# Two-layer attention and MLP block on one core: the place of the memory keys' transposes in the preparation

## The chip, the core and the metric

The kernel runs on one core of a Trainium2 chip, as one launch. The metric is the time of one execution in microseconds (us), the median of three runs. The engines are named as the profile names them: PE (TensorE, matmuls; PEld is its weight load), DVE (VectorE), ACT (ScalarE), POOL (GpSimd) and SP (SyncE, whose queue issues all DMAs of this kernel).

## The reference

The input `x` has 8 batches of 512 tokens of 256 numbers, in float32. Two layers follow each other; each normalises `x` and adds two branches to it:

```python
xn = _layernorm(x)
x = x + attention(xn, Wq, Wk, Wv, pre_proj, post_proj, mem_k, mem_v, Wout, bout) + fp4_mlp(xn, w_gate, w_up, w_down)
xn = _layernorm(x)
x = x + gated_convolution_and_mlp(xn, Wg, Wi, A, Bp, Cp, Dp, gamma, ...) + int4_linear_with_lora(xn, kernel, bias, a, b)
```

The attention has 16 heads of 64. Its keys are 64 learned memory keys per head (`mem_k`) ahead of the tokens' own keys. The dot products of all heads are mixed by `pre_proj` (16x16), masked causally, cut to the 64 largest of each row (`top_k`), put through softmax, mixed by `post_proj`, and applied to the values. The first MLP quantises weights and activations to FP4 in blocks of 16; the second layer's linear part quantises its weight to INT4 with one scale, the maximum over the whole weight.

## The kernel before

The kernel has three stages. The first **prepares weights** and takes the first 117 us. The second, the **search stage**, runs the attention over 64 groups (8 batches times 8 groups of 64 queries) with the selection of the 64 largest keys as a search by counting. The third computes everything else of both layers. A test behind the search stage can send the kernel to an exact, slow path; with these inputs it is not taken.

*How the order is made.* The instructions of a stage are recorded by `Straight` (L165), whose calls all appear as line 235 in the profile, into a `Plan` (L81). `Plan.tails` (L99) gives each operation a due time, minus the costliest chain of work that hangs behind it, plus its `late` mark; `Plan.run` (L114) then places the operations on their engines one after the other by estimated costs, taking the most urgent of those that are ready. What comes out is a fixed order for every engine and for SP; on the chip each engine takes its queue in that order and waits where an operand is missing. `Straight.part` (L185) describes a tile access as one range of partitions and one range of columns, from the first to the last column that it touches; two accesses whose ranges overlap, one of them a write, are taken to depend on each other in the plan. Matmuls that follow each other into one PSUM bank are one operation of the plan. An operation's `after` list names operations that must be placed ahead of it.

*The preparation (L677 to L854).* Its parts are these:

- **Folding (L754 to L782).** The products of `Wq`, `Wk` and `pre_proj` are folded into one matrix `mg` (`mgm` for the memory keys), so that the search stage needs no separate projections. `bd` (L718) holds `Wk` and the memory keys spread in a block pattern of 20 blocks: blocks 0 to 15 hold `Wk`, copied by ACT and DVE, blocks 16 to 19 the transposed memory keys. The loop has 20 turns. Turn `j` has a first product (8 matmuls of `bd[:, c, j]` with `wq` into one of two banks `pa`), a copy to `both` (ACT for even turns, DVE for odd ones), a second product (4 matmuls with `kr`, which holds `pre_proj`, into one of three banks `pm`), a copy to `mg` and a square on ACT, and a sum of the squares on DVE (`sqp`). Turns 16 to 19 use the memory keys. From the sums comes `tot`, which the search stage starts from.
- **Memory keys (L730 to L741).** 8 transposes of `mk` on PE into one bank, and two DVE copies into `bd[rows, :, 16:, t, :]`. Their range of columns, as `part` sees it, reaches from block 16 of the first chunk to the end of the last one, over nearly all of `bd`. They are recorded ahead of the folding loop and marked `late = 30`.
- **First tokens and value weights (L786 to L845).** The first batch is normalised (DVE), transposed (8 on PE), and `Wv` and `Wout` are transposed (32 on PE), marked `late = 4`.
- **`prepare` (L365).** The FP4 weights go through `quantise` eight times, with two sets of tiles (`w_v0` and so on, `w_v1`): two loads of `w_gate` and `w_up` rows by DMA, the largest of each block on DVE (`w_amax`), a product on POOL, ACT and DVE steps, two more products on POOL into `w_lo`, and transposes of `w_lo` on PE. The last two quantise `w_down`. A set's next load waits for POOL's last product on it. The INT4 weight (`kernel`) is loaded into the place of `Wv`, and its maximum goes through one `partition_all_reduce` on POOL (L492), the only library instruction of the stage. Last, `w1s`, weights of the third stage, is stored by DMA (L514); the search stage's first tiles lie where `w1s` lay.

*The search stage's end of a group.* The last round of the search leaves in `raw` minus twice the number of keys above a threshold. L1209 makes `foff` from it on DVE, and `pick` (L1145) compares `foff` with the eight numbers in `io8` (L818) to choose which of the eight largest remaining values is the cut.

Of the kernel before, what the change touches and what calls it, by code (L numbers as in the profile page):

```python
# [11 lines left out]
ALU = mybir.AluOpType  # L12
# [7 lines left out]
H, DH = 16, 64  # L20
HC = H * DH // P
MEM = 64
# [4 lines left out]
GB = 8  # L27
# [15 lines left out]
AIM = LOW + 3.5  # L43
# [22 lines left out]
def keys(ib):  # L66

    return MEM + RB * (ib + 1)
# [528 lines left out]
def block_kernel(ctx: ExitStack, tc: tile.TileContext, a: dict, out: bass.AP):  # L597
    nc = tc.nc
# [4 lines left out]
    ident = const.tile([P, P], F32, name="ident")  # L603
# [42 lines left out]
    with ExitStack() as c0:  # L646
# [15 lines left out]
        io8 = keep.tile([P, 8], F32, name="io8")  # L662
        base = {}
# [13 lines left out]
        with tc.tile_pool(name="prep", bufs=1) as prep, tc.tile_pool(name="prep_ps", bufs=1, space=PSUM) as pps:  # L677
            pl = Plan({})
            r = Straight(nc, pl)
# [3 lines left out]
            def bank(kind):  # L683
                own = {"a": banks[:2], "m": banks[2:5], "t": banks[5:]}[kind]
                used[kind] = used.get(kind, -1) + 1
                return own[used[kind] % len(own)]
# [4 lines left out]
            mk = prep.tile([MEM, H, DH], F32, name="mk")  # L691
# [26 lines left out]
            bd = prep.tile([P, HC, NJ, 2, 16], F32, name="bd")  # L718
            r.gpsimd.memset(bd[:, : HC // 2], 0.0)
            r.vector.memset(bd[:, HC // 2 :], 0.0)  # L720
            for j0 in range(0, 16, 8):
                for t in range(2):
                    for i in range(2):
                        rows = slice(t * DH, (t + 1) * DH)
# [2 lines left out]
                            bd[rows, half, j0 : j0 + 8, t, :],  # L727
                            wkm[rows, half, j0 * 16 : (j0 + 8) * 16].rearrange("p c (j i) -> p c j i", i=16),
                        )
            r.late = 30.0  # L730
            ps = bank("t")
            for c in range(HC):
                r.tensor.transpose(
                    ps[:, c * MEM : (c + 1) * MEM],
                    mk[:, 2 * c : 2 * c + 2, :].rearrange("m h d -> m (h d)"),
                    ident[:MEM, :MEM],
                )
            for t in range(2):
                rows = slice(t * DH, (t + 1) * DH)
                r.vector.tensor_copy(bd[rows, :, 16:, t, :], ps[rows].rearrange("p (c j i) -> p c j i", c=HC, i=16))  # L740
            r.late = 0.0  # L741

            row16 = prep.tile([P, 16], F32, name="row16")
            r.vector.tensor_reduce(row16, ident.rearrange("p (k i) -> p i k", i=16), AX.X, ALU.add)
# [9 lines left out]
            for j in range(NJ):  # L754
                pa = bank("a")
                for i in range(2):
                    for u in range(4):
                        c = 4 * i + u
                        r.tensor.matmul(
                            pa[u * 32 : (u + 1) * 32, i * D : (i + 1) * D], bd[:, c, j].rearrange("p t i -> p (t i)"),  # L760
                            wq[:, c, :], start=True, stop=True,
                        )
                ab = both[j % 3]
                (r.scalar.copy, r.vector.tensor_copy)[j % 2](ab, pa)
                pm = bank("m")
                for e in range(DC):
                    for i in range(2):
                        r.tensor.matmul(
                            pm[:, e * D : (e + 1) * D], ab[:, i * D + e * P : i * D + (e + 1) * P],
                            kr[:, i].rearrange("p k i -> p (k i)"), start=(i == 0), stop=(i == 1),  # L770
                        )
                dst = mg[:, :, :, j * 16 : (j + 1) * 16] if j < 16 else mgm[:, :, :, (j - 16) * 16 : (j - 15) * 16]
                r.scalar.copy(dst, pm.rearrange("p (e k i) -> p e k i", e=DC, i=16))
                r.scalar.activation(junk[j % 2], pm, AF.Square)
                r.vector.tensor_reduce(sqp[:, j], junk[j % 2].rearrange("p (q i) -> p q i", i=16), AX.X, ALU.add)
# [5 lines left out]
            ps = bank("a")  # L781
# [19 lines left out]
            for e in range(DC):  # L801
                ps = bank("t")
# [12 lines left out]
                r.vector.tensor_reduce(cmask[:, c : c + 1], row[:, 0:c], AX.X, ALU.add)  # L815
            r.vector.tensor_scalar(cmask, cmask, MASKED, None, ALU.mult)
            for q in range(8):
                r.gpsimd.memset(io8[:, q : q + 1], 3.5 - q)  # L818
            for na, to in base.items():
                r.gpsimd.memset(to, -2.0 * AIM)  # L820
                for ib in range(NB):
# [6 lines left out]
            for c in range(0, HC, 2):  # L828
                ps = bank("t")
# [6 lines left out]
            for g in range(HC // 2):  # L836
                ps = bank("t")
# [234 lines left out]
        def count(g, s, cur, raw, b, on_act):  # L1072


            src = block(s, g, b)
            thr = cur[:, 0, b : b + 1]
            junk = wp.tile([P, WD[-1]], I8, name=f"junk{int(on_act)}")[:, : src.shape[-1]]
            if on_act:
                nc.scalar.activation(  # L1079
                    junk, src, AF.Sign, bias=thr, scale=-1.0, accum_out=raw[:, b : b + 1]  # L1080
                )
            else:
                nc.vector.scalar_tensor_tensor(  # L1083
                    junk, src, thr, two.to_broadcast([P, src.shape[-1]]), ALU.is_ge,
                    ALU.mult, accum_out=raw[:, b : b + 1],
                )
# [94 lines left out]
        def search(pl, g, s, w, deps, rounds):  # L1181

            def begin():
                w["cur"] = cur = st.tile([P, 2, GB], F32, name="cur", bufs=14)
                nc.gpsimd.tensor_copy(cur[:, 0], guess[:, g * GB : (g + 1) * GB])

            tail = pl.add("POOL", 0.4, begin, deps)
            for k, (na, on_pool) in enumerate(rounds):
                def open_():
                    w["raw"] = st.tile([P, GB], F32, name="raw", bufs=8)  # L1190

                counts = []
                tail = pl.add("none", 0.0, open_, [tail])
                for b in range(GB):
                    def one_count(b=b, na=na):
                        count(g, s, w["cur"], w["raw"], b, b < na)

                    n = keys(g * GB + b)
                    counts.append(
                        pl.add("ACT", 0.28 + 0.00083 * n, one_count, deps + [tail]) if b < na else  # L1200
                        pl.add("DVE", 0.17 + 0.00105 * n, one_count, deps + [tail])
                    )

                def step(k=k, na=na, on_pool=on_pool):
                    if k < len(ROUNDS) - 1:
                        narrow(g, w, k, na, on_pool)
                    else:
                        w["off"] = st.tile([P, GB], F32, name="foff", bufs=4)
                        nc.vector.tensor_scalar(w["off"], w["raw"], -0.5, -AIM, ALU.mult, ALU.add)  # L1209

                last = k == len(ROUNDS) - 1
                tail = pl.add(
                    "POOL" if on_pool else "DVE",
                    0.2 if last else (1.3 if k == 0 else 5.5) if on_pool else 1.8 if k < len(ROUNDS) - 2 else 2.1,
                    step, counts,
                )
                deps = []
            return tail
# [293 lines left out]
        for n, (b, g) in enumerate(groups):  # L1512
# [7 lines left out]
            if n % 2 == 0:  # L1520
                pair = ORDER[n % NG : n % NG + 2]
                q, qdone, stored = queries(pl, pair, o, xdone)
# [4 lines left out]
            w = {}  # L1527
# [55 lines left out]
        with tc.If(flag > 0):  # L1583
            nc.sync.dma_start(mgf, mg_d)
            nc.sync.dma_start(mgmf, mgm_d)
            with tc.For_i(0, B) as b:
# [4 lines left out]
                for n, g in enumerate(ORDER):  # L1591
                    if n % 2 == 0:
                        pair = ORDER[n : n + 2]
                        q, qdone, stored = queries(pl, pair, o, xdone)
# [13 lines left out]
                    w = {}  # L1608
# [21 lines left out]
    r = Straight(nc, pl)  # L1630
# [221 lines left out]
```

## Time and profile before

| | us |
|---|---|
| median of three runs (2841.61 to 2843.36) | 2842.69 |
| the profiled execution | 2840.84 |
| its span, from the first to the last instruction | 2839.1 |
| PE busy, 19064 matmuls | 2539.6 |
| DVE busy, 7978 instructions | 2439.3 |
| ACT busy | 2026.9 |
| POOL busy | 1206.7 |
| the preparation: PE's first instruction of the search stage starts at | 117.28 |
| PE, DVE and POOL busy in 0 to 117.28 | 79.87, 79.55 and 40.87 |
| DVE busy, L1209 (64 instructions) | 11.3 |

The profile is one execution seen by a hardware profiler. A row of its timeline gives the start, the length, the engine, the line, the operation, the tiles written and read, and how often it is repeated; in brackets stands how long the engine had been idle before it and what ended that idle time. "SPq" rows are DMAs being issued. A row of windows gives, for a stretch of time, each engine's busy time and its number of instructions.

### The profile page before, as it was taken

The numbers are of one execution on the slowest core, as the hardware profiler recorded it, in microseconds if no ns is written. First come the engines' busy times: TensorE is split into PE (matmuls) and PEld (weight loads), VectorE is DVE, ScalarE is ACT, GpSimd is POOL, SyncE is SP. The second block draws the span as 40 slices with busy tenths as digits, with TensorE's granted clock in tenths as the row PEclk, the third lists the DMA queues.
The fourth block names the chain that finished last, engine by engine and source line by source line (L and its number), as shares of the span: only waits on it lengthen the run. The fifth ranks groups of instructions, "written<-read, shape, count | busy, mean of one in ns | idle before, by whom it ended". The sixth has DMA issues, their size and how long they took to land. (4 is left out here: it accounts for less than half of the span.)

```text
span 2839.1 us, 57481 instructions
## 1 busy us (share of the span) xinstructions
PE 2539.6 (89%) x19064; PEld 1966.9 (69%) x19064; DVE 2439.3 (86%) x7978; ACT 2026.9 (71%) x5876; POOL 1206.7 (43%) x2215
## 2 busy tenths in 40 slices
PE   5999999999999999999999999999986578999997
PEld 3677777777777778777787777778765455666664
DVE  6678989989989998999899889999999969877762
ACT  3478887788788878887888788788897444644442
POOL 3203544345444544444453545455445344444320
PEclk9999999999999999999999999999987788999998
DMA  4300010100000000000000010000110031000000
GB/s 135 148 24 16 27 30 16 29 18 19 21 25 18 28 18 27 20 18 26 21 19 18 25 29 17 16 23 20 35 42 5 8 109 30 23 16 15 8 8 15
DMA packets 114871, 82.70 MB, mean 29 GB/s; under 512 B 79339, under 2 KB 108806, under 8 KB 113798
## 3 DMA queue, kind: packets, MB, share of 16 engines
q1 hardware_dynamic: 114566, 78.95, 9.1%
q8 instruction: 153, 2.51, 0.4%
q14 instruction: 152, 1.25, 0.1%
HBM read 44.04 MB, written 35.39 MB: 28 GB/s over the span
## 5 line engine op out<-in xcount | busy, mean ns | idle before, releaser
L1079 ACT ACTIVATE junk<-ring,cur 128x312 int8<-128x312 f32 (+27 forms) x1560 | 864.0, 560 | 32.9 <-POOL cur L1132 12.0
L1083 DVE SCALAR_TENSOR_TENSOR junk<-ring,cur,two 128x72 int8<-128x72 f32 (+9 forms) x1512 | 828.0, 580 | 19.7 <-POOL cur L1132 17.7
L1037 PE MATMUL ps_sc<-xnT,tk 128*128 128x8 f32 (+38 forms) x2048 | 536.4, 408 | 37.3 <-ACT ring L1043 36.9
L997 PE MATMUL ps_mi<-rows,mg 128*128 128x128 f32 x4096 | 501.9, 277 | 10.5 <-ACT tk L1008 10.5
L997 PEld LDWEIGHTS ps_mi<-rows,mg 128*128 128x128 f32 x4096 | 480.5, 192 | 39.0 <-issue 13.8
L1037 PEld LDWEIGHTS ps_sc<-xnT,tk 128*128 128x128 f32 x2048 | 348.4, 199 | 185.8 <-issue 89.8
L1283 PE MATMUL ps_at<-mixd,ring 128*128 128x128 f32 (+1 forms) x3072 | 410.4, 284 | 63.1 <-POOL mixd L1260 58.5
L1283 PEld LDWEIGHTS ps_at<-mixd,ring 128*128 128x128 f32 (+1 forms) x3072 | 365.1, 185 | 96.0 <-POOL mixd L1260 72.4
L1167 DVE SCALAR_TENSOR_TENSOR ring<-ring,kth,e 128x520 f32<-128x520 f32 (+56 forms) x512 | 276.1, 561 | 86.2 <-ACT e L1158 84.1
L1099 POOL TENSOR_TENSOR cur<-base,raw 128x8 f32<-128x8 f32 x186 | 50.1, 269 | 658.7 <-ACT junk L1079 626.8
L1079 ACT ACTIVATION_READ_ACCUMULATOR junk<-ring,cur 128x1 f32 x1560 | 303.5, 195 | 0.0
L1289 ACT COPY at<-ps_at 128x512 f32<-128x512 f32 (+1 forms) x384 | 221.9, 581 | 101.5 <-PE ps_at L1283 98.3
L1140 DVE SCALAR_TENSOR_TENSOR y<-ring,cur 128x520 f32<-128x520 f32 (+56 forms) x512 | 288.7, 564 | 3.1
L1043 ACT COPY ring<-ps_sc 128x456 f32<-128x456 f32 (+56 forms) x512 | 184.4, 374 | 125.0 <-PE ps_sc L1037 120.4
L1143 DVE MAX8 top<-y 128x8 f32<-128x520 f32 (+56 forms) x512 | 255.3, 499 | 17.6
L1158 ACT ACTIVATE e<-ring 128x520 f32<-128x520 f32 (+56 forms) x512 | 228.2, 472 | 19.6 <-DVE ring L1167 19.4
L1307 PE MATMUL ps_y<-at,v 128*64 128x64 f32 (+1 forms) x6144 | 225.3, 225 | 16.9 <-ACT at L1289 16.8
L1307 PEld LDWEIGHTS ps_y<-at,v 128*64 128x64 f32 (+1 forms) x6144 | 198.7, 138 | 55.7 <-ACT at L1289 31.6
L1122 POOL TENSOR_TENSOR by<-gap,minus 128x8 f32<-128x8 f32 x124 | 220.5, 1779 | 9.7
L1008 ACT COPY tk<-ps_mi 128x256 f32<-128x256 f32 x512 | 168.0, 377 | 59.4 <-PE ps_mi L997 58.7
L1260 POOL TENSOR_TENSOR mixd<-mix,rden 128x512 f32<-128x512 f32 x128 | 153.1, 1212 | 132.8 <-DVE rden L1252 85.2
L235 PE MATMUL ps_gu<-mg,ring 128*128 128x352 f32 x448 | 148.8, 477 | 15.2 <-DVE hid L235 10.3
(316 smaller groups left out, 3934.7 us busy)
## 6 DMA issues: line engine op xcount, KB each, us to landing
msd<-scr SPq DMA_DIRECT2D x32, 512.0 KB
ring<-msd SPq DMA_DIRECT2D x512, 32.0 KB
scr<-in_L_attn_x_dram SPq DMA_DIRECT2D x10, 512.0 KB
mg_d<-mg SPq DMA_DIRECT2D x1, 4096.0 KB
att<-o SPq DMA_DIRECT2D x64, 64.0 KB
ring<-in_L_attn_x_dram SPq DMA_DIRECT2D x8, 512.0 KB
ring<-att SPq DMA_DIRECT2D x8, 512.0 KB
out_dram<-ring SPq DMA_DIRECT2D x8, 512.0 KB
```

The lines of the kernel that those rows point to most:

```text
L997: nc.tensor.matmul(ps[:, j * P : (j + 1) * P], mg[:, e, k + j, e2 * P : (e2 + 1) * P], toks(e), start=(e == 0), stop=(e == DC - 1),)
L1037: nc.tensor.matmul(ps[:, :ntok], q["tk"][side_of(g)][e][:, b].rearrange("p k i -> p (k i)"), o["xnT"][:, e, :ntok], start=(e == 0), stop=( ...
L1079: nc.scalar.activation(junk, src, AF.Sign, bias=thr, scale=-1.0, accum_out=raw[:, b : b + 1])
L1083: nc.vector.scalar_tensor_tensor(junk, src, thr, two.to_broadcast([P, src.shape[-1]]), ALU.is_ge, ALU.mult, accum_out=raw[:, b : b + 1],)
L1122: eng.tensor_tensor(by, gap[:, 1], minus, ALU.pow)
L1140: nc.vector.scalar_tensor_tensor(y, src, cur[:, 0, b : b + 1], src, ALU.is_ge, ALU.subtract, reverse1=True)
L1143: nc.vector.max(out=top[:, b, :], in_=y)
L1158: nc.scalar.activation(e, src, AF.Exp, scale=1.0 / SMALL)
L1167: nc.vector.scalar_tensor_tensor(src, src, kth[:, b : b + 1], e, ALU.is_ge, ALU.mult, accum_out=den[:, b : b + 1])
L1283: nc.tensor.matmul(pt[:n, b * P : (b + 1) * P], s[:, 4 * j + b, col : col + n], w["mix"][j][:, b, :], start=True, stop=True,)
L1289: nc.scalar.copy(ats[c][:n, :, j * 4 * RB : (j + 1) * 4 * RB].rearrange("p k (b i) -> p b k i", i=RB), w.pop(("pt", c, j))[:n].rearrange(" ...
L1307: nc.tensor.matmul(w["py"][j * DH : (j + 1) * DH, q * GR : (q + 1) * GR], vs[c][:n, k * DH : (k + 1) * DH], ats[c][:n, k, :], start=(c == ...
```

## The change

The 8 transposes of the memory keys and their two copies are no longer recorded ahead of the folding loop with `late = 30`, but inside it, in turn `j == 9`, between the turn's copy to `both` and its second product, without a `late` mark. The transposes are also told to be placed after that copy. In a second part, the last round's `foff` is made by one tensor-by-tensor subtraction from `base[0]` (64 columns of -2 * AIM) instead of by one multiply-and-add with constants; the numbers in `foff` and `io8` are both doubled by this, so that the comparison chooses the same value.

```diff
-            r.late = 30.0
-            ps = bank("t")
-            for c in range(HC):
-                r.tensor.transpose(
-                    ps[:, c * MEM : (c + 1) * MEM],
-                    mk[:, 2 * c : 2 * c + 2, :].rearrange("m h d -> m (h d)"),
-                    ident[:MEM, :MEM],
-                )
-            for t in range(2):
-                rows = slice(t * DH, (t + 1) * DH)
-                r.vector.tensor_copy(bd[rows, :, 16:, t, :], ps[rows].rearrange("p (c j i) -> p c j i", c=HC, i=16))
-            r.late = 0.0
...
-                (r.scalar.copy, r.vector.tensor_copy)[j % 2](ab, pa)
+                op = (r.scalar.copy, r.vector.tensor_copy)[j % 2](ab, pa)
+                if j == 9:
+
+                    ps = bank("t")
+                    for c in range(HC):
+                        mk_op = r.tensor.transpose(
+                            ps[:, c * MEM : (c + 1) * MEM],
+                            mk[:, 2 * c : 2 * c + 2, :].rearrange("m h d -> m (h d)"),
+                            ident[:MEM, :MEM],
+                        )
+                    mk_op.after.append(op)
+                    for t in range(2):
+                        rows = slice(t * DH, (t + 1) * DH)
+                        r.vector.tensor_copy(
+                            bd[rows, :, 16:, t, :], ps[rows].rearrange("p (c j i) -> p c j i", c=HC, i=16)
+                        )
...
-                r.gpsimd.memset(io8[:, q : q + 1], 3.5 - q)
+                r.gpsimd.memset(io8[:, q : q + 1], 7.0 - 2 * q)
...
-                        nc.vector.tensor_scalar(w["off"], w["raw"], -0.5, -AIM, ALU.mult, ALU.add)
+                        nc.vector.tensor_tensor(w["off"], base[na][:, g * GB : (g + 1) * GB], w["raw"], ALU.subtract)
```

## The prediction, as it was put on record

> **What bounds the kernel now.** The change touches the preparation and one small DVE instruction per group. Behind the preparation the recorded order of every engine is the same in both kernels, so I read the preparation's end and carry the shift through. First the windows: PE has 79.87 us of work before 117.28, and 28.6 us of its 37.4 us of idle time lie ahead of 37.20.
>
> ```profile
> core 0: us, PE busy (x) PEld busy (x) DVE busy (x) ACT busy (x) POOL busy (x), PEclk, DMA share, GB/s
> 0.00:16.30 16.30, 0.00 (x0) 0.01 (x1) 14.47 (x35) 7.45 (x10) 10.80 (x70) 1.00 0.91 264
> 16.30:37.20 20.90, 8.58 (x40) 6.49 (x40) 10.26 (x24) 4.27 (x9) 7.38 (x59) 1.00 0.73 209
> 37.20:57.90 20.70, 18.44 (x169) 11.90 (x168) 12.45 (x28) 9.86 (x19) 6.15 (x6) 1.00 0.13 40
> 57.90:95.00 37.10, 33.00 (x247) 22.37 (x248) 26.64 (x55) 19.05 (x35) 9.67 (x8) 0.95 0.07 22
> 95.00:117.28 22.28, 19.85 (x153) 14.70 (x152) 15.72 (x33) 9.45 (x28) 6.86 (x5) 1.00 0.81 341
> ```
>
> PE's waits up to 122 us say why: it waits for the memory keys' load, then in queue order for the copies into `bd` and for the first tokens.
>
> ```profile
> PE pps L235 <- DMA mk<-in_L_attn_mem_k_dram: 16.3, 1, 16.3
> PE pps L235 <- DVE scr L235: 6.0, 1, 6.0
> PE pps L235 <- DVE bd L235: 4.6, 1, 4.6
> PE pps L235 <- DVE vt L235: 4.0, 1, 4.0
> PE pps L235 <- DVE both L235: 2.3, 1, 2.3
> ```
>
> The timeline gives the chain: the second load of `w_v` holds DVE to 30.45, and behind it stands the tokens' scaling; folding starts at 37.22. At the end the store of `w1s` goes out, and POOL and ACT start the search stage when it has landed. That store is what the preparation ends with.
>
> ```profile
> 10.50 2.50 ACT L235 COPY bd<-ring 64x512 f32<-64x512 f32 x4 [0.44 <-DMA ring<-in_L_attn_Wk_dram]
> 30.45 0.69 DVE L235 TENSOR_REDUCE w_amax<-w_v 128x32 f32<-128x512 f32 x1 [7.21 <-DMA w_v<-in_L_ffn_w_up_dram]
> 37.23 1.93 PE L235 MATMUL pps<-ring,bd 128*32 128x256 f32 x32
> 43.59 0.86 POOL L235 PARTITION_ALL_REDUCE mxa<-mx  x1 [6.72 <-DVE w_lo L235]
> 51.52 0.72 POOL L235 TENSOR_TENSOR bsum<-bsum,b 128x256 f32<-128x256 f32 x1 [7.06 <-ACT junk L235]
> 66.73 3.52 PE L235 MATMUL pps<-ring,both 128*128 128x256 f32 x8
> 71.67 1.89 PE L235 MATMUL pps<-ring,both 128*128 128x256 f32 x8
> 116.90 0.32 SPq L235 DMA_DIRECT2D w_d<-w1s  x1
> 121.89 0.40 POOL L955 COPY rows<-xnT 128x256 f32<-128x256 f32 x1 [10.81 <-DMA w_d<-w1s]
> ```
>
> **What moves.** The old copies' range covers nearly all of `bd`, so the plan made all 20 turns wait for the keys. Now only turns 10 to 19 do. The chain behind `Wk` and `Wq` becomes the most urgent, and the two orders compared show this: SP issues `Wk`, `Wq` and `pre_proj` first, ahead of the four first `w_v` loads, the tokens, `Wv`, the keys and `Wout`; PE starts with 8 first and 6 second products of turns 0 to 7, then the rest of turns 8 and 9, and only then the keys' 8 transposes, the tokens' 8 and 32 of `Wv` and `Wout`. No instruction is added. SP also issues five loads (`la`, `lb`, `mem_v`, `bout`, `por`) ahead of the second `w_v` loads instead of behind or among them, and the loads into `Wv`'s place (`kernel` among them) behind them.
>
> **The sum, by PE's queue.**
>
> *Start.* In the old trace `Wk`, 1 MB behind 1 MB of other loads, had landed at 10.50, where ACT's copies begin; now the first 2 MB are `Wk` and `Wq`. I take 9 (8 to 10.5).
>
> *Work before the first stall.* From the rows a first product takes 1.00 and a second 1.92 at full pace (49.72, 50.72, 52.64): 8 x 1.00 + 6 x 1.92 = 19.5, and 1.9 more for a cold start (behind PE's pause of 4 us at 62: 3.52 against 1.89 in the rows at 66.73 and 71.67, and 0.73 against 0.42 for the four transposes ahead of them). So 9 + 21.4 = 30.4, when PE needs DVE's copy of turn 7.
>
> *Stall.* That copy stands on DVE behind the second `w_v` loads. These landed for DVE at 30.45; the five loads now ahead of them add their issue times, 0.43 + 0.46 + 0.66 + 0.43 + 0.57 = 2.55: 33.0 (30.4, if SP catches up, to 35). Behind it two `w_amax` (0.69 each), scales (0.5), a `sqp` (0.67), the scaling of the tokens (1.46) and the copy (0.68): 4.7. PE goes on at 37.7. At that time PE stood at the start of folding before, with 40 transposes done; now 19.5 us of folding are done.
>
> *The rest.* PE's 79.87 us contain two cold stretches: the 40 transposes took 8.58, at 0.109 each at full pace (0.42 for four at 36.63) 4.3; and 1.9 at 66. That leaves 79.87 - 4.3 - 1.9 = 73.7, of which 54.2 remain. To it come: 1.9 for the cold restart; 2 for the middle, where `w_lo` comes late because POOL's reduction does (0 to 8; near the 1.0 that PE waited for POOL's `w_lo` before); 5 for the last turns, where DVE does both `w_down` quantisations (11.6 us by the 704-wide rows, 0.52 to 0.89 each) ahead of the copy of turn 19 and PE has 7 us beside it, and 1.9 for the cold stretch behind that; 1.5 as at the old end (waits of 1.0 and less). End: 37.7 + 54.2 + 1.9 + 2 + 6.9 + 1.5 = 104.2, against 117.28: **13.1 us less**.
>
> The big stores of `mg` and the weights go out earlier too, so `w1s` lands as it did, 5 us behind its issue, and the search stage starts 13.1 us sooner with the same order.
>
> *`foff`.* 64 of a mean of 176 ns (11.3 us). The nearest rows of the new kind, 128x8 tensor by tensor on DVE, have means of 163 (L1129) to 238 ns (L1099, the same operands right behind the counts): -0.8 to +4.0 us. Medians are alike (170 and 166), so I take 0 and keep 4.0 in the range. The 8 memsets of `io8` are as before.
>
> The profiled execution goes from 2840.84 to 2827.7; it lies 1.85 below the median, so the median goes from 2842.69 to **2829.6**.
>
> **Rivals.**
>
> [...] POOL stood idle 6.72 ahead of the reduction and 7.06 behind it, with nothing to wait for in the second. If the first pause counts from the arrival of its operand, it is no longer hidden. `mx` is now late, since `kernel` is loaded behind `Wv`'s transposes: about 47 by the step below. Then `w_lo` and PE behind it slip by 6.7, and 13.1 becomes 6.4: 2836.3. For the forecast speaks that the pause is as long as the second one, counted from POOL's last memset at 36.87, not from `mx` (39.5), and in the new order about 10 us lie between the two. [...]
>
> *The lead is given back.* If the quantisations' chain through DVE and POOL sets the end, and not PE's queue, the early turns buy nothing: 2842.7, no change.
>
> *Slower.* One step of that chain gets later. The third `w_v` loads leave at 53.50, 63.4 ahead of the `w1s` store, when POOL has done `w_lo`, behind the reduction. By the new order `kernel` is issued when PE has done two first products, a second one and 32 transposes from 37.7 on: 2.0 + 1.9 + 3.5, and 1.9 as it is cold, or 47.0. Then 2.2 to land (as from 53.88 to DVE's `w_amax` at 56.13), `mx` 0.7, reduction 0.9, pause 7.1, two products 2.3: 60.2, or 6.7 later. If the 63.4 stay, the kernel takes 2849.4. It decides if POOL and DVE are the limit behind the third load. Against it: from 57.90 on POOL is busy 16.5 of 59.4 us and DVE 42.4, while PE is busy 52.9.
>
> **Chances.** Forecast 0.60 (its own range 2825 to 2834), library 0.15, lead given back 0.11, slower 0.07, and 0.07 that more is won (2822: no stall in the middle, loads as early as before). A measurement can tell about 0.2%, 5.7 us, from no change: faster 0.60 + 0.07 + 0.10 of the library's 0.15 = 0.77; same 0.16; slower 0.07. The range takes in the library case, and leaves out the slower one and most of the lead given back: 2822 to 2840.
>
> **What would show it.** Right: folding's first product near 9 us; DVE's second `w_amax` near 33 and PE idle ahead of it by 6 to 9; the store of `mg` near 75 to 80 instead of 95.22; POOL's `rows` near 108 to 110 instead of 121.89; the span behind it as long as before, and L1209 near 170 ns. Wrong: PE idle for over 5 us between 45 and 75 behind POOL (library), `w1s` stored at 115 or later, or a search stage that is longer by what the preparation lost.

## The result, and the profile after

| | before | after | predicted |
|---|---|---|---|
| median of 8 runs, us | 2842.76 (2840.61 to 2846.22) | 2835.30 (2828.39 to 2837.25) | 2829.6 (2822 to 2840) |
| ratio to before | | 0.9970, 95% interval 0.9960 to 0.9981 | 0.9954 |
| profiled execution, us | 2840.84 | 2836.09 (span 2834.4) | 2827.7 |
| `w1s` stored, us | 116.90 | 108.11 | 103.8 |
| POOL's `rows`, us | 121.89 | 112.11 | 108 to 110 |

The kernel became faster by 7.5 us, as forecast in direction, and by 0.57 of the 13.1 us forecast. The time lies in the range. The profile says that the preparation won 9.8 us (112.11 against 121.89) and that the profiled execution kept only 4.8 of them. So two things have to be explained: 3.3 us less in the preparation than I had worked out, and a loss in a search stage whose recorded order did not change.

The windows of the changed kernel, cut at PE's two long waits (columns as in the prediction's table):

```profile
0.00:8.05 8.05, 0.00 (x1) 0.04 (x2) 6.34 (x14) 1.95 (x3) 6.65 (x88) 1.00 0.74 251
8.05:29.65 21.60, 21.54 (x176) 13.68 (x176) 16.78 (x37) 11.98 (x21) 8.17 (x37) 1.00 0.86 241
29.65:36.11 6.46, 0.00 (x0) 0.00 (x0) 4.99 (x13) 1.63 (x3) 1.74 (x2) 0.85 0.52 174
36.11:85.08 48.97, 46.90 (x370) 32.57 (x370) 39.65 (x81) 27.57 (x51) 17.09 (x14) 0.95 0.29 104
85.08:90.55 5.47, 0.00 (x0) 0.02 (x1) 5.47 (x11) 1.86 (x4) 1.80 (x1) 0.84 0.93 400
90.55:108.06 17.51, 15.96 (x60) 12.12 (x60) 8.05 (x22) 5.44 (x19) 5.78 (x5) 0.66 0.32 130
```

PE starts at 8.05 and works 21.5 us before its first wait; it waits 6.5 us and 5.5 us, both for DVE's copies, and in the last 17.5 us it is busy at a granted clock of 0.66. That last row is the one to remember: PE hardly waits there (it is busy for 15.96 of 17.51 us), it is slow. (The record of the clock starts near 13.7 us. The 1.00 printed for the time ahead of it is no measured value: PE's first 32 products took 3.75 us, against 1.93 for the 32 at 14.63.)

The timeline of the changed kernel, with the rows that answer to those shown of before, and two of the search stage:

```profile
8.05 3.75 PE L235 MATMUL pps<-ring,bd 128*32 128x256 f32 x32 [8.05 <-DVE bd L235]
30.95 0.69 DVE L235 TENSOR_REDUCE w_amax<-w_v 128x32 f32<-128x512 f32 x1 [5.71 <-DMA w_v<-in_L_ffn_w_up_dram]
36.12 3.64 PE L235 MATMUL pps<-ring,bd 128*32 128x256 f32 x32 [6.47 <-DVE both L235]
49.61 0.38 POOL L235 PARTITION_ALL_REDUCE mxa<-mx  x1 [12.10 <-DVE mx L235]
56.69 1.73 POOL L235 TENSOR_TENSOR w_lo<-w_lo,w_v 128x512 f32<-128x512 f32 x1 [6.70 <-ACT mg L235]
90.56 3.75 PE L235 MATMUL pps<-ring,both 128*128 128x256 f32 x8 [5.49 <-DVE both L235]
108.11 0.32 SPq L235 DMA_DIRECT2D w_d<-w1s  x1
112.11 0.40 POOL L958 COPY rows<-xnT 128x256 f32<-128x256 f32 x1 [15.62 <-DMA w_d<-w1s]
112.56 5.47 PE L971 MATMUL ps_mi<-mgm,rows 128*128 128x512 f32 x8 [1.90 <-POOL rows L958]
329.91 5.41 PE L1334 MATMUL ps_y<-woT,y 128*128 128x256 f32 x16 [2.77 <-ACT y L1324]
```

The same two pieces of the search stage in the timeline of the kernel before (its lines are numbered 3 lower):

```profile
122.34 3.70 PE L968 MATMUL ps_mi<-mgm,rows 128*128 128x512 f32 x8 [1.75 <-POOL rows L955]
338.13 3.72 PE L1331 MATMUL ps_y<-woT,y 128*128 128x256 f32 x16 [2.75 <-ACT y L1321]
```

Eight products take 5.47 us instead of 3.70, and sixteen take 5.41 instead of 3.72 behind a pause of the same length (2.77 and 2.75). The work is the same; the pace is not. Here is where the lead goes. I matched the instructions of the two traces in order. At `rows` the changed kernel is 9.8 us ahead; behind the first of these rows 8.0, and 8.2 soon after; behind the second 6.6; and behind a third slow place, at 379 us, 5.1. From there to the 57th of the 64 groups the distance stays at 5.0 within 0.3 us. Three slow places make 1.8 + 1.6 + 1.5 = 4.9 of the 5.0 us that the profiled execution lost.

The other side of this comparison matters as much. Behind `rows` each engine runs the same sequence of instructions in all 14 traces of this case (only the form of `foff` differs), and of these the kernel before has the shortest time from `rows` to the end: 2717.2 us, against 2722.3 in the changed kernel and up to 2726.3 in e4 below. So the 5.0 us are a distance from the luckiest of the 14, and no run shows them as a price of the change.

### The profile page after: what moved, and what is told of

The parts are those of the page before. It is cut to its first block, busy times and chain, and to the rows that moved or that the text cites. A ratio compares the mean times of both kernels' runs of the same rounds, so it can differ in the third digit from the quotient of the medians.

```text
span 2834.4 us, 57481 instructions
## 1 busy us (share of the span) xinstructions
PE 2544.3 (90%) x19064; PEld 1970.1 (70%) x19064; DVE 2443.0 (86%) x7978; ACT 2028.8 (72%) x5876; POOL 1209.9 (43%) x2215
## 5 line engine op out<-in xcount | busy, mean ns | idle before, releaser
L1161 ACT ACTIVATE e<-ring 128x520 f32<-128x520 f32 (+56 forms) x512 | 228.0, 472 | 19.6 <-DVE ring L1170 19.4
L1310 PE MATMUL ps_y<-at,v 128*64 128x64 f32 (+1 forms) x6144 | 225.3, 225 | 17.2 <-ACT at L1292 16.9
```

Of the source, the lines that this page charges most:

```text
L1161: nc.scalar.activation(e, src, AF.Exp, scale=1.0 / SMALL)
L1310: nc.tensor.matmul(w["py"][j * DH : (j + 1) * DH, q * GR : (q + 1) * GR], vs[c][:n, k * DH : (k + 1) * DH], ats[c][:n, k, :], start=(c == ...
```

## The experiments

Each ran beside the kernel before on the same chip; e1 to e4, e5 to e8, e9 to e11 and e12 had four different chips, so between these groups, and with the changed kernel (0.9970, interval 0.9960 to 0.9981), only the ratios can be compared. The times are medians. "Store" is the issue of `w1s`, at 116.90 in the kernel before and at 108.11 in the changed one; "rows" is POOL's `rows`, which starts when that store has landed, at 121.89 and 112.11. Store and `rows` are of one execution each.

| kernel | first folding product | store | rows | median (runs' range) | ratio, 95% interval |
|---|---|---|---|---|---|
| e1 move of the keys alone | 8.01 | 107.13 | 112.89 | 2834.97 (2832.0 to 2838.4) | 0.9968 (0.9956 to 0.9980) |
| e2 `foff` alone | 36.67 | 115.74 | 120.73 | 2844.23 (2838.3 to 2851.2) | 1.0001 (0.9990 to 1.0011) |
| e3 keys' part of `bd` in its own tile | 34.89 | 116.26 | 121.24 | 2846.75 (2843.6 to 2849.4) | 1.0007 (0.9997 to 1.0016) |
| e4 before, `Wk` and `Wq` urgent | 25.22 | 109.65 | 114.63 | 2840.53 (2838.1 to 2842.7) | 0.9984 (0.9975 to 0.9993) |
| e5 keys behind turn 15 | 7.99 | 128.76 | 132.76 | 2854.63 (2852.5 to 2859.8) | 1.0045 (1.0031 to 1.0059) |
| e6 keys behind turn 7 | 8.44 | 103.69 | 109.84 | 2832.12 (2829.8 to 2833.5) | 0.9964 (0.9952 to 0.9976) |
| e7 turn 19's copy on ACT | 8.27 | 109.98 | 113.98 | 2836.11 (2834.5 to 2840.4) | 0.9976 (0.9967 to 0.9985) |
| e8 PE busy through its wait | 8.01 | 109.98 | 113.97 | 2834.58 (2831.2 to 2838.3) | 0.9973 (0.9964 to 0.9982) |
| e9 keys' transposes in another bank | 27.16 | 110.62 | 115.64 | 2841.00 (2838.5 to 2842.9) | 0.9988 (0.9979 to 0.9997) |
| e10 e9 with `Wk`, `Wq` urgent | 8.01 | 99.70 | 104.81 | 2832.87 (2824.9 to 2833.7) | 0.9956 (0.9943 to 0.9968) |
| e11 e6, small loads held back | 8.44 | 99.51 | 105.68 | 2828.09 (2824.0 to 2831.9) | 0.9941 (0.9928 to 0.9954) |
| e12 e10, small loads held back | 8.02 | 99.61 | 103.75 | 2827.47 (2820.2 to 2830.2) | 0.9930 (0.9916 to 0.9943) |

### Which half of the change: e1 and e2

```diff
 e1 = changed kernel, and
-nc.vector.tensor_tensor(w["off"], base[na][:, g * GB : (g + 1) * GB], w["raw"], ALU.subtract)
+nc.vector.tensor_scalar(w["off"], w["raw"], -0.5, -AIM, ALU.mult, ALU.add)
-r.gpsimd.memset(io8[:, q : q + 1], 7.0 - 2 * q)
+r.gpsimd.memset(io8[:, q : q + 1], 3.5 - q)
 e2 = kernel before with the opposite edit
```

> The changed kernel with the old foff (scalar form) and the old io8 values, so only the move of the keys' transposes is left. The foff instructions have a median of 166 ns in the changed kernel and 170 ns in the kernel before, 64 of them, and nothing waits for them in the trace. Theory: the move makes the whole difference, the time is that of the changed kernel, 2835.3 (its runs lie between 2828 and 2837), and the stage that prepares the weights ends where it does there: w1s stored at 108.1, POOL's rows at 112.1. Rival: foff in its new form costs up to 3 us of the search stage, since 3 of the 5 us that are lost behind the preparation are lost in groups 5 to 8: then 2832 or less, with the same preparation.

> The kernel before with the new foff (tensor by tensor) and the new io8 values only. Theory: nothing, 2842.8 within 2 us, w1s stored at 116.9. Rival that the foff edit brings the gain: 2835. Rival that it costs 3 us: 2846.

The move alone gives the whole difference, and `foff` alone gives none that the runs can tell: ratios of 0.9968 against the changed kernel's 0.9970, and 1.0001 with an interval of some 3 us either way. In the traces `foff` has a median of 166 ns in its new form and 170 in its old one, and nobody waits for it. The term of 0 in the sum was right.

### Why folding starts early: e3, e4, e9

The prediction gave a cause: the copies' range in `bd` covered all turns, so all turns waited for the keys. e3 takes away that overlap and nothing else.

```diff
-bd = prep.tile([P, HC, NJ, 2, 16], F32, name="bd")
+bd = prep.tile([P, HC, 16, 2, 16], F32, name="bd")
+bk = prep.tile([P, HC, NJ - 16, 2, 16], F32, name="bk")
... (bk is cleared as bd is)
-    r.vector.tensor_copy(bd[rows, :, 16:, t, :], ps[rows].rearrange("p (c j i) -> p c j i", c=HC, i=16))
+    r.vector.tensor_copy(bk[rows, :, :, t, :], ps[rows].rearrange("p (c j i) -> p c j i", c=HC, i=16))
... (turns 16 to 19 read bk)
```

> The kernel before, with the keys' part of bd (turns 16 to 19) in a tile of its own; the keys' transposes and their late mark stay where they were. Two more memsets, no other instruction. Theory of the prediction (the copies' range covers nearly all of bd, so all 20 turns wait for the keys; without that overlap the chain behind Wk and Wq starts first): folding's first product near 8 to 10, w1s stored at 108 or earlier, 2828 to 2836. Rival (the overlap is not what held folding back; Wk and Wq become urgent only because the keys' transposes, now recorded behind turn 9, stand ahead of all other users of the three transposing PSUM banks, so that everything recorded behind them hangs on turn 9): the order of the first loads stays as in the kernel before, with Wk and Wq behind the tokens, Wv and Wout, folding starts at 33 to 37, and the time is 2842.8 or more; with the turns ordered anew around the same late start, up to 11 us more.

The timeline of e3:

```profile
3.16 0.51 SPq L235 DMA_DIRECT2D ring<-in_L_attn_Wv_dram  x1
4.51 2.21 SPq L235 DMA_DIRECT2D ring<-in_L_attn_Wout_dram  x1
6.77 2.42 SPq L235 DMA_DIRECT2D ring<-in_L_attn_Wk_dram  x2
34.89 3.76 PE L235 MATMUL pps<-ring,bd 128*32 128x256 f32 x32 [10.13 <-POOL w_v L235]
116.26 0.32 SPq L235 DMA_DIRECT2D w_d<-w1s  x1
```

The overlap is gone and nothing is won: `Wk` is loaded even later, behind `Wv` and `Wout`, the keys' transposes still stand first in PE's queue, and folding starts at 34.89. **As the cause of the early loads, the overlap that the prediction named falls.**

e4 goes the other way: the overlap stays, and only the order of the loads is that of the changed kernel.

```diff
+r.late = -100.0
 for i in range(2):
     half = slice(i * HC // 2, (i + 1) * HC // 2)
     r.sync.dma_start(wkm[:, half], ...)
...
     r.sync.dma_start(wq[:, half], ...)
+r.late = 0.0
 r.sync.dma_start(mk, ...)
```

> The kernel before, with the loads of Wk, pre_proj and Wq marked 100 more urgent for the planner, so that SP issues its loads in the order of the changed kernel; the overlap in bd and the place of the keys' transposes are as before, so all turns still wait for the keys. Theory that the false wait on the keys is what cost the time: the keys' load is now the eleventh-odd instead of the eighth-odd, PE waits for it until 16 to 18 and folding starts no earlier than 24; what the early part gains is 12 us at most, and with the quantisations as they were the end moves by 0 to 8: 2835 to 2843. Theory that the order of the first loads brings the whole gain: w1s stored at 108, 2835. Rival that the order of loads brings nothing alone: 116.9 and 2842.8.

Folding starts at 25.22, behind the keys, and `rows` comes at 114.63: 7.3 us of the 9.8 that the whole change wins there come with the early loads alone, although folding starts 17 us later than in the changed kernel. So most of what the early turns could bring is lost somewhere in the changed kernel.

The remaining candidate is the PSUM banks. The three banks of kind "t" are handed out in turn, in recorded order, and each user waits for the one that had the same bank before. In the changed kernel the keys' transposes are recorded behind turn 9 and ahead of all other users. Counted in the listing, the users that get their bank behind them are two of the four groups of `Wv`'s transposes, one of `Wout`'s and those of the first quantised weights, so these hang on turn 9. With them hang the load of `kernel` into `Wv`'s place, and the third quantisation, which writes the first one's tile `w_lo`, with all that follows in that tile. (The tokens' transposes get other banks.) That lengthens the chain behind `Wk`, and the planner makes it the most urgent. e9 moves those transposes to a bank of the second products and keeps all else.

```diff
 if j == 9:
-    ps = bank("t")
+    ps = bank("m")
```

> The changed kernel, keys' transposes behind turn 9 as there, but into one of the three banks of folding's second products instead of the three transposing banks. Turns 0 to 9 still need no keys. Theory of the bank order: the users of the transposing banks no longer hang on turn 9, Wk and Wq lose their urgency, SP issues the tokens, Wv and Wout ahead of them again (the order of loads shows this), folding starts near 30, w1s is stored at 113 to 118 instead of 108.1: 2839 to 2845. The prediction's theory (turns 0 to 9 start early since they need not wait for the keys): as the changed kernel, 2835.

The timeline of e9:

```profile
3.71 0.58 SPq L235 DMA_DIRECT2D ring<-in_L_attn_Wout_dram  x1
4.34 1.85 SPq L235 DMA_DIRECT2D ring<-in_L_attn_Wk_dram  x2
27.16 2.57 PE L235 MATMUL pps<-ring,bd 128*32 128x256 f32 x32
43.25 0.60 PE L235 MATMUL pps<-ident,w_lo 128*128 128x128 f32 x4
63.46 1.11 PE L235 MATMUL pps<-ident,mk 64*128 64x64 f32 x8
110.62 0.32 SPq L235 DMA_DIRECT2D w_d<-w1s  x1
```

With the bank alone changed, the early start is gone: `Wk` is behind `Wout` again, folding starts at 27.16, the time is 2841.0. The quantised weights' transposes (43.25) now stand ahead of the keys' (63.46); in the changed kernel they stood behind them (52.11 behind 39.69). The store came 2.4 us earlier than the earliest that I expected (113); the keys no longer stand at the head of PE's queue, which may be the reason.

### What hangs on the bank: e5, e6, e10

> The changed kernel with the keys' transposes behind turn 15 instead of turn 9; nothing else. Only turns 16 to 19 then need the keys. Theory after the first four runs: the users of the three transposing PSUM banks go in recorded order, so the transposes of Wv, Wout and all quantised weights stand behind the keys' transposes, and with them the load of kernel, the third w_v loads and the w_down loads. Six more turns ahead of them are 6 x 2.9 = 17.5 us of PE: the w_down loads leave near 90 instead of 73.1, the 5.5 us of PE's wait ahead of turn 19 go, and w1s is stored at 118 to 126 instead of 108.1: 2846 to 2855. The prediction's theory (what counts is how many turns need the keys): no change or a little better, 2833 to 2835.

> The changed kernel with the keys' transposes behind turn 7 instead of turn 9. Theory of the bank order: what stands behind the keys' transposes moves up by two turns, 5.8 us: third w_v loads at 52 to 54 (58.5), w_down loads at 66 to 68 (73.1), w1s stored at 101 to 104 (108.1), 2828 to 2831. Rival that PE's own work or DVE's quantisations set the end whatever the place: w1s at 107 to 108, 2835. Rival of the prediction that each turn which need not wait for the keys counts: 2 turns more wait, 2835 to 2838.

e5 and e6 change one number, the turn behind which the keys stand (`if j == 9` to 15 and to 7). The timeline of e5:

```profile
56.29 0.71 PE L235 MATMUL pps<-ident,mk 64*128 64x64 f32 x8
68.76 1.04 PE L235 MATMUL pps<-ident,w_lo 128*128 128x128 f32 x8
96.16 3.01 SPq L235 DMA_DIRECT2D w_v<-in_L_ffn_w_down_dram  x2
128.76 0.32 SPq L235 DMA_DIRECT2D w_d<-w1s  x1
```

and of e6:

```profile
25.56 0.71 PE L235 MATMUL pps<-ident,mk 64*128 64x64 f32 x8
44.89 1.09 PE L235 MATMUL pps<-ident,w_lo 128*128 128x128 f32 x8
70.91 3.52 SPq L235 DMA_DIRECT2D w_v<-in_L_ffn_w_down_dram  x2
103.69 0.32 SPq L235 DMA_DIRECT2D w_d<-w1s  x1
```

In both, what stands behind the keys moves with them: at turn 7, 9 and 15 the keys are transposed at 25.56, 39.69 and 56.29, the weights at 44.89, 52.11 and 68.76, and the store goes out at 103.69, 108.11 and 128.76. In e5 PE then waits for the late quantisation. Of its waits up to 133 us the longest in total (us, times, longest) is

```profile
PE pps L235 <- POOL w_lo L235: 28.2, 4, 14.0
```

More turns without the keys made the kernel slower, against the prediction's cause: at turn 15 by some 20 us, so that it is slower than the kernel before. At turn 7 only the preparation shows a gain, and a smaller one than the store says: the stores ahead of `w1s` go out right before it there, it lands 6.2 us behind its issue instead of 4.0, and `rows` is 2.3 us earlier. In the time the ratios 0.9964 and 0.9970 cannot be told apart. I had put the `w_down` loads too early in both (expected near 90 and at 66 to 68), and e5's store as well (118 to 126).

e10 has e9's bank and e4's urgent loads, so both reasons for an early start hold and nothing hangs on turn 9.

> As e9_bank_m, and the loads of Wk, pre_proj and Wq marked 100 more urgent. Theory: early loads, no wait of the early turns for the keys, and nothing hung on turn 9 is more than each part alone: third w_v loads near 53, w1s stored at 100 to 104, 2828 to 2832. Rival: early loads are worth what they are in e4_wk_first whatever the keys do: w1s at 109.7, 2840.

```profile
8.01 3.85 PE L235 MATMUL pps<-ring,bd 128*32 128x256 f32 x32 [8.01 <-DVE bd L235]
45.80 1.04 PE L235 MATMUL pps<-ident,w_lo 128*128 128x128 f32 x8
50.55 0.71 PE L235 MATMUL pps<-ident,mk 64*128 64x64 f32 x8
99.70 0.32 SPq L235 DMA_DIRECT2D w_d<-w1s  x1
```

In e10's timeline folding starts as early as in the changed kernel, the `w_down` loads leave 6.1 us earlier (66.98 against 73.11), the store goes out 8.4 us earlier and `rows` comes 7.3 us earlier (104.81 against 112.11). That is what hanging on turn 9 costs the preparation in these two traces: of 17.1 us that early loads and early turns win at `rows`, 7.3 are given back because the weights' transposes, and with them the later loads into the same tiles, wait for turn 9. How much of it is pace these two traces do not part from the rest: in its last stretch the changed kernel has four windows at half clock (0.50 from 88.84, 92.25, 99.08 and 102.49). In the time this price is not shown: the intervals of the ratios, 0.9943 to 0.9968 and 0.9960 to 0.9981, overlap.

Against e4, where the loads are as early and all turns wait for the keys, e10 wins 9.8 us more at `rows` (104.81 against 114.63), and the intervals of the ratios do not meet. So the wait for the keys ahead of the first turns does cost time once `Wk` is loaded early; it is only not what made `Wk` early.

### The last stretch: e7, e8, and the pace of PE

```diff
 e7
-op = (r.scalar.copy, r.vector.tensor_copy)[j % 2](ab, pa)
+op = (r.scalar.copy, r.vector.tensor_copy)[j % 2 if j < 19 else 0](ab, pa)
 e8
 pm = bank("m")
+if j == 19:
+    for i in range(14):
+        spin = r.tensor.matmul(pm[:, :D], wq[:, i % HC, :P], wq[:, i % HC, :], start=True, stop=True)
+    spin.cost = 0.0
```

> The changed kernel with the copy of turn 19 on ACT, which is free there, instead of DVE, where it stands behind 11.9 us of w_down quantisation. Theory that PE's 5.5 us of waiting for that copy are on the path: w1s stored at 102.6, 2830. Theory that the quantisation of w_down through DVE and POOL sets the end (POOL's last w_lo ends at 96.44, and DVE is freed of a copy of 0.68 only): PE's wait moves behind the product of turn 19 and stays as long, half pace follows it all the same, w1s at 106.5 to 107.5, 2834 to 2835.

> The changed kernel with 14 more products of 128x256 (0.22 us each) into the bank of turn 19's second product, which that product overwrites: PE works through its wait for the copy. They are 3.1 us in a wait of 5.5 and are on nobody's path. Theory that the half pace behind that wait costs 5 us of the preparation (its last 17.5 us hold 16.0 us of PE work, which is some 11 at full pace) and 1.8 of the first products of the search stage: no half pace from 88 to 117, w1s stored at 103 to 105, rows at 107 to 109, 2829 to 2832. Rival that the quantisation's end at 96.4 leaves no room: w1s at 107 or later and 2835. [...]

Freeing the copy does not win back PE's second wait. In e7 the copy no longer stands behind DVE's quantisation, and PE waits as long, now for POOL's `w_lo`:

```profile
96.16 1.54 PE L235 MATMUL pps<-ident,w_lo 128*128 128x128 f32 x6 [6.59 <-POOL w_lo L235]
109.98 0.32 SPq L235 DMA_DIRECT2D w_d<-w1s  x1
```

The store has to be read from PE's restart behind the first wait, since that differs from run to run (36.12 in the changed kernel, 38.89 in e1, 39.18 in e7, 37.28 in e8). From there it is 72.0 us in the changed kernel, 68.2 in e1, 70.8 in e7 and 72.7 in e8.

e8 failed: PE worked without a gap to 94.3, and the store was not earlier. Two things can hold it, and e8 does not part them. POOL's last `w_lo` ends 60.7 us behind PE's restart (60.3 in the changed kernel), so the quantisation leaves no room, as the rival has it. And in the windows of e8, cut where the clock changes, half pace comes behind the next thin stretch instead:

```profile
93.79:97.20 3.41, 2.16 (x16) 1.50 (x14) 1.68 (x3) 2.00 (x7) 3.33 (x3) 1.00 0.36 151
97.20:100.62 3.42, 3.10 (x16) 3.00 (x17) 1.72 (x6) 2.02 (x7) 0.79 (x2) 0.50 0.37 156
100.62:104.03 3.41, 3.41 (x13) 3.05 (x14) 1.14 (x7) 0.77 (x4) 0.00 (x0) 0.50 0.15 56
```

What the pace costs is best seen in two traces with the same order on PE. The changed kernel, in steps of 3.41 us from 88.84:

```profile
92.25:95.67 3.42, 3.34 (x11) 2.35 (x10) 1.72 (x3) 1.83 (x6) 3.34 (x3) 0.50 0.00 0
95.67:99.08 3.41, 2.87 (x23) 2.48 (x24) 1.55 (x6) 2.18 (x9) 0.82 (x2) 1.00 0.73 308
99.08:102.49 3.41, 3.41 (x13) 2.96 (x13) 1.56 (x9) 0.69 (x4) 0.00 (x0) 0.50 0.27 107
102.49:105.91 3.42, 3.42 (x10) 2.23 (x8) 0.21 (x2) 0.63 (x2) 0.00 (x0) 0.50 0.43 164
```

and e1, from 90.09:

```profile
93.50:96.92 3.42, 3.42 (x10) 2.60 (x10) 2.96 (x4) 0.67 (x2) 3.34 (x3) 0.50 0.10 43
96.92:100.33 3.41, 2.67 (x22) 2.13 (x20) 0.64 (x4) 2.27 (x10) 1.98 (x3) 1.00 0.64 269
100.33:103.74 3.41, 3.30 (x22) 2.85 (x22) 2.59 (x11) 1.55 (x7) 0.00 (x0) 1.00 0.17 68
103.74:107.16 3.42, 2.40 (x12) 1.47 (x10) 1.32 (x4) 0.74 (x2) 0.00 (x0) 1.00 0.62 241
```

Both PE queues restart with turn 19's second product, at 90.56 and at 93.06, and both run it at half pace. Then e1 gets full pace and reaches the search stage's first product at 107.09, 14.0 us later; the changed kernel gets two more windows of half pace and needs 17.5. The order is the same, so these 3.5 us are only pace. At `rows` 1.7 us of them are left (19.8 us from the restart in e1 and 21.6 in the changed kernel), as `w1s` lands 5.8 us behind its issue in e1 and 4.0 in the changed kernel.

### A version that is faster than both: e11, e12

e6 and e10 still show the first wait, for the second `w_v` loads. Both were given an order in which the five small loads that the prediction had counted (`la`, `lb`, `mem_v`, `bout`, `por`) are held behind them.

```diff
... (the five loads and the loads of w_v are kept in lists)
+for op in small_ops + r.small:
+    op.after += r.loads[4:8]
```

> e6_turn7 with the five small loads (la, lb, mem_v, bout, por) held behind the second w_v loads. These five take 2.5 us of SP ahead of the loads that DVE waits for. Theory (the prediction's step on the stall): DVE's w_amax at 28 to 29.5 instead of 31.45, and what follows moves with it: w1s stored at 100.5 to 102.5 instead of 103.7, 2829 to 2831. Rival: the loads are limited by what is ahead of them in the DMA queue and not by their issue: w_amax at 31 to 32 and 2832.

> e10_bank_m_wk (keys behind turn 9 in a bank of the second products, Wk, pre_proj and Wq marked urgent) with the five small loads held behind the second w_v loads as in e11_turn7_loads. Theory: the two gains add, as they lie in different waits: e11 took 4.2 us off the w1s store of e6, so w1s is stored at 95.5 to 97.5 instead of 99.7 and the time is 2826 to 2830. Rival: with the bank free the second w_v loads are no longer what holds DVE and PE: w1s at 99 to 100, 2832.

The `w_amax` of the second loads in e6 and in e11:

```profile
31.45 0.69 DVE L235 TENSOR_REDUCE w_amax<-w_v 128x32 f32<-128x512 f32 x1 [4.67 <-DMA w_v<-in_L_ffn_w_up_dram]
29.40 0.69 DVE L235 TENSOR_REDUCE w_amax<-w_v 128x32 f32<-128x512 f32 x1 [2.39 <-POOL bsum L235]
```

In e11 it starts 2.0 us earlier, and the store goes out at 99.51 instead of 103.69. In e12 the quantisations are 1.8 us earlier all along (`w_down` loads at 65.19 against 66.98 in e10), but the store is not (99.61, where I expected 95.5 to 97.5); what held it is not shown. At `rows` 1.1 us are left (103.75 against 104.81). The ratios of the two, 0.9941 and 0.9930, have intervals that overlap, and neither can be called the faster. Both intervals lie below the changed kernel's: e11 and e12 are faster than it, by some 8 and 11 us.

## Why the prediction was right and where it was wrong

**Start, first work, first stall: right, and a little too long.** Folding started at 8.05 (9), PE's first wait began at 29.65 (30.4) and ended at 36.12 (37.7); the second `w_v` loads reached DVE at 30.95 (33.0). In four traces with this order they arrived between 30.95 and 34.02, so the 2.0 us in my favour are luck, within what a run varies. That the five loads ahead of them cost about 2 us agrees with two pairs of traces (31.45 and 29.40 in e6 and e11, 31.89 and 29.92 in e10 and e12), one execution each.

**The middle: right.** From 36.11 to 85.08 PE was idle 2.1 us (2), and the first products behind the cold restart cost 1.7 more (1.9): 3.64 us for the 32 at 36.12, against 1.93 for the 32 at 14.63.

**The last turns: the wait right, the pace wrong.** PE waited 5.5 us (5). The term that was mis-sized is "1.9 for the cold stretch behind that". With 9.2 us of work left at full pace (54.2 and 1.9, less the 46.9 done by 85.08), 1.9 and 1.5, I had 12.6 us; it took 17.5. Half pace held not for a first stretch only but in four of the six windows from 88.84 to 109.32, and in the next two, at the start of the search stage. PE's work there is thin, short pieces that wait for POOL and ACT; but that alone does not decide, since e1 ran the same pieces at full pace behind its first stretch and took 14.0. The 1.6 us by which PE restarted early and the 1.0 by which `w1s` landed sooner (4.0 us behind its issue, not 5) hid part of the miss.

**The search stage: I gave it no term.** I wrote that it starts sooner "with the same order", and that the span behind `rows` stays as it is. It grew by 5.0 us in the profiled execution, 4.9 of them in three places at half pace. The order is the same, as I wrote; what I left out is that its time is not. By my count over the 14 traces the time from `rows` to the end follows the number of 3.41 us windows at half pace in its first 1828 us, some 55 of the 64 groups: 14.0 windows in the kernel before (2717.2 us), 15.0 in e1 (2719.3), 17.2 in the changed kernel (2722.3), 18.0 to 19.4 in e4, e5, e7 and e9 to e12 (2723.3 to 2726.3). A straight line through the 14 points has 1.5 us for each window and leaves 1 us or less. Over the medians the loss is smaller: 9.8 us won at `rows`, 7.5 in the time.

**The cause of the order was wrong, the sum did not need it.** The step that failed is "The old copies' range covers nearly all of `bd`", taken as the reason why the chain behind `Wk` and `Wq` becomes the most urgent. I took the changed order from the two orders side by side, and that order is what ran. But e3 shows that to take the overlap away alone is worth nothing, and e9, e5 and e6 that the bank which the moved transposes take sets both the urgency of `Wk` and what comes late. Who had gone by my cause would have put the keys behind turn 15, and lost 11 us to the kernel before. That the time fell into the range owes nothing to this cause.

**The rivals.** *The all-reduce's pause ("library" in the chances):* no. No run shows a library being loaded; what they show is POOL's idle time around the reduction. It started at 49.61, 0.1 us behind the end of `mx` (48.78 + 0.69), so the pause ahead of it did not count from its operand; the pause behind it (6.70) held `w_lo` up by 0.9 at most, as its operand was done near 55.8. That this rival's 2836.3 lies nearest to the time is a coincidence. *Lead given back:* in part, by another way than I had thought; against e10 it is 7.3 us at `rows`. *Slower, by late third loads:* they did leave late (58.45 against 53.50, I had 60.2), but the 63.4 us from there to the store shrank to 49.7; folding was done sooner (`mg` stored at 76.25, not 95.22), so less of it shared PE and DVE with the quantisations.

**Still open:** how the windows at half pace are spread over the runs of one kernel. The profiled execution of e4, 2842.68, is the slowest of its eleven and has the most of them (19.4), so it keeps nothing of its 7.3 us; e10 and e11 have medians 4.8 us apart, but intervals that overlap and profiled executions of 2830.3 and 2831.9. A profile shows one execution only, and what the other runs had is not on record.

## What to carry to other kernels

Where a planner orders the work, ask of a moved step not only what it reads and writes but what it takes: a PSUM bank handed out in recorded order ties its later users, and what waits for them, to the place where the step now stands, and here the preparation won 7.3 us more, in one trace each, with another bank and an urgent mark on the loads that start the chain (e10). Test a cause by removing it alone (e3) before building on it. And if a change moves a long stage by a few us without touching it, the time need not follow in full: here 9.8 us at `rows` became 4.8 in the profiled execution, and in the three places that took the rest PE ran at half clock behind pauses of 1.9 to 2.8 us, in one trace and not in the other. Count the windows at half clock in both traces before looking for another reason, and remember that the trace of before can be the lucky one.

## What the runs showed of the hardware

In the traces of the kernel before and of the changed kernel the granted clock of PE was 1.00 or 0.50 and nothing between, and its stretches, but for the last, were multiples of 3.41 us. Half clock came also behind a window in which PE had work: from 327.78 to 331.19 of the changed kernel it was busy 1.28 of 3.41 us, and the next window ran at 0.50:

```profile
327.78:331.19 3.41, 1.28 (x6) 1.16 (x7) 3.33 (x9) 3.41 (x13) 0.81 (x3) 1.00 0.01 2
331.19:334.60 3.41, 3.41 (x10) 2.70 (x9) 3.34 (x9) 3.41 (x13) 0.00 (x0) 0.50 0.01 2
```

How long PE was busy in a window, and at which clock the next one ran, I counted in the same two traces (1647 windows of 3.41 us). At full clock, all 54 windows with PE busy for less than 1.4 us were followed by half clock, of 25 with 1.4 to 1.8 us 6, and of 1431 with more 6. At half clock, where 32 first products took 3.64 us (at 36.12) and not 1.93, all 57 windows with less than 2.6 us stayed at half, and 54 of the 57 with 3.4 us were followed by full clock. The few that differ are not explained: with 2.87 us busy, in short pieces, the one from 95.67 of the changed kernel was followed by half clock, and the one of 2.67 us from 96.92 of e1 was not.

The same pause of 2.8 us was followed by half clock in one execution and not in the other (5.41 and 3.72 us for the 16 products behind it). In the kernel before, PE was busy 1.54 us in the window from 336.25, which holds the pause's end, and the next one stayed at 1.00; in the changed kernel that window, from 327.78, has the 1.28 us above. Whether this makes the spread of the runs of one kernel (2820.2 to 2830.2 in e12) is not shown, as only one run of each has a trace.

The second `w_v` loads, issued in the same order, reached DVE at 30.95, 32.12, 33.73 and 34.02 us in four traces (changed kernel, e8, e1 and e7). The store of `w1s` landed (POOL's `rows` starts then) 4.0 to 6.2 us behind its issue, latest in e6 and e11, where 1 MB and two smaller stores had left in the 4.4 us ahead of it. And where the operand of POOL's all-reduce was ready early, the reduction started 5.4 to 6.4 us behind POOL's instruction before it (e3, e4, e6, e9, e10, e12).
